# Attention in blocks of four tokens, with gated loads and three loads a pair on GpSimd, in a four-layer kernel

## The chip, the cores and the metric

The kernel runs on one core of a Trainium2 chip. The core has TensorE (PE: matrix products; PEld is its loading of stationary operands), VectorE (DVE), ScalarE (ACT), GpSimd (POOL) and SyncE (SP), each with an instruction queue of its own that runs in order, and 16 DMA engines that move data between HBM and the on-chip memory SBUF. Products land in PSUM, eight banks of 128 x 512 floats. The metric is device time in microseconds. All data is fp32.

## The reference

The input `x` is 64 sequences of 64 tokens with 256 features, 4,096 tokens in all. Four layers follow, each added to its input:

```python
# 0: two projections with weights scaled by the sequence's condition
down = relu(einsum('bsd,bdh->bsh', x, down_project * dg + db))
x = x + (einsum('bsh,bhd->bsd', down, up_project * ug + ub) + x)
# 1: a weight per sequence, of rank 30, made by a decoder
U = (mu @ W_dec + b_dec).reshape(B, 257, 30)
x = x + (x @ (U @ V)[:, :-1] + (U @ V)[:, -1:])
# 2: attention among the 16 heads of one token, q = k = v
kx = modulated_linear(x, ...).reshape(B, N, 16, 16)
A = softmax(einsum('bnhd,bnjd->bnhj', kx, kx) / 4)
x = x + modulated_linear(einsum('bnhj,bnjd->bnhd', A, kx).reshape(B, N, 256), ...)
# 3: norms with gathered gains, three state vectors, an MLP over six parts, a norm
x = x + mlp_ln(concat([w0*h, w1*t, w2*m, w3*n, w4*r, w5*s]), ...)
```

In layer 2 every token has its own 16 x 16 table of scores between its heads. So attention is 4,096 small products of 16 x 16 by 16 x 16, and the same number with the values.

## The kernel before

Layers 0, 1 and the keys of layer 2 go over chunks of 512 tokens (eight, `layers01`); attention and everything behind it go over pairs of 128 tokens, that is 256 (sixteen, called P; `attention` and `layers23`). Activations are kept with features in the partitions up to the keys (`xs`, `kT`).

**How attention is packed.** TensorE transposes the keys of a pair (`pt`, L721), ScalarE copies them twice into `kk` (L727 with feature ahead of head, L730 as they are), and SP writes both forms to HBM, `kd` (L736) and `vd` (L744). From there `fetch` brings them back in other arrangements:

- `kc` (L754) holds a row for each of 16 features and 8 groups of 32 tokens, 128 rows. ScalarE copies it into `kz`, where every token's 16 columns lie between zeros (L756).
- `kb` (L762, eight loads, one a group) is block-diagonal: the rows of group b are filled in block b only, and the other blocks stay zero. `vb` (L767, eight loads) is the same for the values.

A product of `kz`'s 32 columns for one g by `kb[:, :, g, :]`, 8 blocks of 16 columns, so takes eight tokens at once; two of them accumulate, since the 32 columns are a window that holds the tokens in one half (L789). This is `pS`: 32 products of 128 x 32 by 128 x 128 a pair, spread over the four 32-column groups of the array, four partitions' quarters of one PSUM bank. Of each product's output 16 rows count, and the accumulation fills both halves.

VectorE then takes the maximum over each row (L796) and subtracts it (L797), ScalarE takes the exponential (L798), VectorE sums (L799), inverts (L800), multiplies (L801) and transposes in 32 x 32 blocks into `at` (L803). `pv` is 32 products of `at`'s 32 columns by `vb[:, :, g, :]`, again 128 columns (L813), in two banks; ScalarE copies each into `av` (L818), and `av` goes to HBM (`ad`, 512 KB, L822) and comes back as `aT` with features in the partitions (L829). Rows that hold another token's product are left behind there. The tokens arrive in an order of their own, which `styleq` (L502) and the output's copy `ot` (L886) follow.

`kb` and `vb` are there once, `kz` twice. They lie in `kv`, which at the start holds layer 1's decoder (`W_dec`, six pieces); once the decoder is used up, GpSimd fills `kv` with zeros (L488, two halves).

**The norms.** `layers23` gathers rows of three tables with indirect loads on GpSimd (L856, six a pair) and loads `ei`, `tab` and `xr`, the parked residual, on SP (L861, L862, L871). Each of three norms a pair takes a power of -0.5 on GpSimd (L842), between a VectorE instruction (L841) and those that use it (L906, L920, L959).

**The start.** All weights are loaded once. SP issues nearly all of them in the order of their use, ScalarE the six pieces of the decoder. `pU` (L469, 60 products) makes the factor `U` from the decoder; VectorE adds the bias (L472).

**The order of instructions.** No engine chooses at run time. Every piece of work is a `step` with an engine, an estimated cost, what it reads and writes, and a rank; `Plan.order` plays the steps against a simple model of the engines and emits them in the order of their modelled starts. The rank is a base, by pair or chunk, plus a number for the step's stage (`LEAD`) and one by stage and pair (`SHIFT`). So a change of these two tables reorders every queue. A step whose buffer is still in use can't be placed earlier than the buffer's modelled release. On the chip, each instruction waits for what it needs, and all that stand behind it on its engine wait with it.

Of the kernel before, what the change touches and what calls it, by code (L numbers as in the profile page):

```python
# [19 lines left out]
CH = 512  # L20
# [41 lines left out]
class Plan:  # L62
# [6 lines left out]
    LEAD = {"down": 946.4, "fetch": 1090.6, "gather": 1168.5, "hidden": 1056.4, "keys": 938.1, "last": 1046.3,  # L69
            "load": 934.3, "load W1": 1568.6, "load W2": 1287.4, "load decoder": 1245.0, "load first": 604.2, "load ids": 902.1,  # L70
            "load keys": 911.3, "load states": 1260.1, "load up": 753.0, "mid": 546.9, "norm": 984.7, "out": 1165.7,
            "park": 927.1, "scores": 1120.2, "set W1": 1041.3, "set decoder": 215.9, "set down": 150.6, "set k": 952.6,
            "set o": 868.6, "set states": 1178.6, "turn": 1040.2, "up": 1091.5, "values": -313.8}


    SHIFT = {"down": (121.0, 0.0, -136.0, 0.0, 45.3, 0.0, 57.2, 0.0, 669.8, 0.0, 452.8, 0.0, 448.6, 0.0, 203.0, 0.0),
            "fetch": (-21.2, -95.4, 22.4, 39.5, 73.9, 129.8, -198.4, 143.2, 60.9, 236.7, -128.9, -10.1, -60.7, 22.7, -201.3, -74.5),
            "gather": (25.1, 20.6, -52.3, 44.9, 149.5, 295.4, 273.6, -73.2, 25.2, 4.2, 71.4, 347.0, 156.9, 181.1, 284.4, 233.7),
            "hidden": (-23.7, -102.8, 100.9, 97.4, -70.1, 56.9, 93.3, -244.5, -119.8, 73.4, -11.9, 193.5, 100.1, -16.4, -8.7, 2.5),
            "keys": (-138.5, 0.0, -157.5, 0.0, 320.2, 0.0, 194.1, 0.0, 169.5, 0.0, 259.2, 0.0, 207.7, 0.0, 209.6, 0.0),  # L80
            "last": (-49.6, -146.3, 100.1, 60.6, -162.7, -187.0, 32.8, 25.1, 68.0, -10.7, 96.6, -194.4, -61.8, 407.3, 397.6, 375.4),
            "load": (0.0, 0.0, 0.0, 0.0, 311.2, 0.0, 24.7, 0.0, -364.5, 0.0, 23.9, 0.0, 66.9, 0.0, 299.3, 0.0),
            "mid": (-25.3, 0.0, -351.6, 0.0, -179.2, 0.0, -1.1, 0.0, -6.1, 0.0, 131.7, 0.0, 213.3, 0.0, 249.5, 0.0),
            "norm": (-246.5, -272.7, -139.3, -283.8, -207.2, -15.7, -104.9, 40.1, -219.1, 16.5, -133.9, -101.4, -119.9, 129.5, 13.2, -265.9),
            "out": (75.9, 13.0, -112.7, -113.3, -174.2, 11.1, 82.9, 26.4, 125.1, -118.1, 220.2, -0.8, 136.4, 254.8, -8.3, 195.2),
            "park": (-302.5, 0.0, -53.5, 0.0, -775.7, 0.0, -547.9, 0.0, -550.1, 0.0, -359.8, 0.0, -152.5, 0.0, 238.3, 0.0),
            "scores": (-82.8, 70.4, 67.7, -137.7, -106.8, -38.2, 26.9, 83.3, 98.4, 82.9, 84.9, -0.6, 136.4, 144.2, 34.2, 171.0),
            "turn": (-82.0, 10.3, -20.8, -18.4, -23.5, -0.8, 77.8, 214.9, 84.7, 115.0, -41.3, 77.4, -122.1, 45.8, 69.3, 164.8),
            "up": (-344.7, 0.0, -102.1, 0.0, -238.6, 0.0, -224.7, 0.0, -115.4, 0.0, -84.9, 0.0, -54.9, 0.0, -53.0, 0.0),
            "values": (-74.2, 53.7, -70.1, -159.6, 81.8, 307.5, -59.3, -54.8, 80.6, -145.4, -166.2, -196.3, -101.8, -85.7, -218.8, 125.5)}  # L90
# [12 lines left out]
    @staticmethod  # L103
    def keys(things):
        out = []
        for t in things:
            if isinstance(t, tuple) and isinstance(t[0], Buf):
                out.append((t[0], t[1]))
            else:
                out.append((t, None))  # L110
        return out
# [142 lines left out]
def act(n):  # L254
    return 0.06 + n / 1220.0
# [3 lines left out]
def tile_kernel(ctx: ExitStack, tc: tile.TileContext, a: dict, out: bass.AP):  # L259
# [15 lines left out]
    BUFS = {"x": 3, "xr": 3, "pw": 2, "cg": 2, "mg": 2, "ei": 2, "oh": 2, "t4": 3, "kk": 2, "kc": 1, "act": 2, "E": 2,  # L275
            "aT": 2, "xt": 2, "ft": 2, "hs": 2, "y3": 2, "y1": 1, "mx": 2, "sm": 2, "tab": 2, "st": 2, "mv": 2, "rs": 2, "rsx": 2, "rsh": 2, "rsy": 2, "nmx": 2, "nmh": 2}
# [4 lines left out]
    def bank(name, tag="B"):  # L281
        return Buf(ps, tag, {"A": 2, "B": 3, "C": 2, "S": 1}[tag], [128, 512], name, turns=(tag == "A"))
# [35 lines left out]

    styleq = fixed("styleq", [128, 2, B // PB, 4, 2])
# [14 lines left out]
    kz = [fixed(f"kz{i}", [128, 32 * NG + 16]) for i in range(2)]  # L334

    kv = fixed("kv", [128, 2 * NG * 128])
    kb, vb = (kv[:, i * NG * 128 : (i + 1) * NG * 128].rearrange("p (b g j) -> p b g j", g=NG, b=8) for i in range(2))
    at_ = fixed("at", [128, 32 * NH + 16])


    def consts():
# [4 lines left out]
    step("POOL", 0.4, lambda: (nc.gpsimd.memset(neghalf, -0.5), nc.gpsimd.memset(V, 0.0), nc.gpsimd.memset(bigtab, 0.0),  # L346
                               nc.gpsimd.memset(at_[:, 32 * NH :], 0.0)),
         w=["neghalf", "V", "at0", "zeros"], rank=-107)
    step("POOL", 3.5, lambda: nc.gpsimd.memset(U, 0.0), w=["U"], rank=-108.5)
    for z in range(2):  # L350
        step("POOL", 1.0, lambda z=z: nc.gpsimd.memset(kz[z], 0.0), w=[f"kz{z}"], rank=-106)
# [5 lines left out]
    def load_x(c, rank):  # L357
        x = xs_[c] = sb("x", [128, 2, CH], f"x_{c}")
        step("SP", Plan.ISSUE, lambda: nc.sync.dma_start(x(), xTd[:, :, c * CH : (c + 1) * CH]),
             w=[(x, 0), (x, 1)], rank=rank, dma=4 * 128 * 2 * CH)  # L360
# [35 lines left out]
    load_x(1, -109.1)  # L396
# [3 lines left out]
    for i, (n, tag) in enumerate((("h", "ft"), ("t", "ft"), ("m", "fs"), ("n", "fh"), ("r", "aS"), ("s", "ot"))):  # L400
        W1r[n] = sb(tag, [128, 2, D], f"W1r_{n}")
    plan.stage = "load W1"
    for i, n in enumerate("htmnrs"):
        step("SP", Plan.ISSUE, lambda i=i, n=n: nc.sync.dma_start(W1r[n](), int_W1[i]), w=[W1r[n]], rank=-108.5 + 0.01 * i, dma=262144)
    plan.stage = "load states"
    load("cond64T", cond64T, a["cond64T"], -108.4)
    load("fsideT", fsideT, a["fsideT"], -108.4)
    rows_, w1_, w2_ = {}, {}, {}
    rowsd = a["rows"].rearrange("(m v) d -> m (v d)", m=3)
    for i, (m, kdim, t2, tr) in enumerate((("mem", C, "xt", "av"), ("noi", 64, "xt", "cg"), ("res", 32, "xh", "pw"))):  # L410
# [3 lines left out]
        step("SP", Plan.ISSUE, lambda m=m: nc.sync.dma_start(w1_[m](), a[f"{m}_W1"]), w=[w1_[m]], rank=-108.3, dma=1024 * kdim)  # L414
        step("SP", Plan.ISSUE, lambda m=m: nc.sync.dma_start(w2_[m](), a[f"{m}_W2"].rearrange("(k p) o -> p k o", p=128)),
             w=[w2_[m]], rank=-108.2, dma=262144)
        step("SP", Plan.ISSUE, lambda m=m, i=i: nc.sync.dma_start(rows_[m]()[0:B, 0 : 3 * D], rowsd[i].partition_broadcast(B)),
             w=[rows_[m]], rank=-108.1, dma=196608)
    betas = fixed("betas", [128, 3, 2, 8])
    load("betas", betas, a["betas"].rearrange("n (k p) e -> p n k e", p=128), -108.0)  # L420
    plan.stage = "load W2"
    load("W2", W2, a["int_W2"].rearrange("(k p) o -> p k o", p=128), -107.9)
    load("irow", irow, a["int_rows"].rearrange("n d -> (n d)").partition_broadcast(128), -107.8)
# [63 lines left out]
    for n, half in (("kb", 0), ("vb", 1)):  # L487
        step("POOL", 3.5, lambda half=half: nc.gpsimd.memset(kv[:, half * NG * 128 : (half + 1) * NG * 128], 0.0),  # L488
             w=[n] + [f"W_dec{i}" for i in range(NW)], rank=-104)


    for n in "ko":
# [8 lines left out]
        if n == "o":  # L501
            step("DVE", 1.0, lambda: [nc.vector.tensor_copy(  # L502
# [268 lines left out]
    def parts(n):  # L771
        return [f"{n}.{b}" for b in range(8)]
# [274 lines left out]
```

## Time and profile before

| | |
|---|---|
| median of nine runs | 489.71 us (480.35 to 496.4) |
| profiled execution | 484.41 us |
| its span, first to last instruction | 482.6 us |
| TensorE's granted clock, mean | 0.932 |
| packets moved by DMA | 192,668, 83.53 MB |
| DMA queue of SP (q1) | 51.6% of 16 engines' span |
| DMA queue of GpSimd (q0) | 15.9% |

The time of a run lies a little above the span. Lines of the profile name the source line, the engine and the operation, the tile written and those read. "Idle before" is the time for which the engine had nothing to do ahead of an instruction, with what ended it. SPq, ACTq and POOLq are the parts of those engines that issue DMAs; time there is issuing, not moving. A matrix product in fp32 appears as two records. The granted clock (PEclk) is a share of full speed.

### The profile page before, as it was taken

How to read it: one execution, taken by the hardware profiler on the slowest of the kernel's cores; microseconds unless marked ns; L12 is line 12 of the kernel's file. 1: busy time of each engine (PE TensorE's matmuls, PEld its weight loads, DVE VectorE, ACT ScalarE, POOL GpSimd, SP SyncE). 2: the span in 40 equal slices, each digit the busy share in tenths (PEclk: the TensorE clock that was granted, in tenths of full speed). 3: DMA queues.
4: the chain of work that ended last, by engine and by line, in shares of the span. 5: the costliest groups of instructions: out<-in, count | busy, mean ns of one | idle time of the engine just before them, and what ended most of it. 6: DMA issues, size and time to landing. Idle time of an engine off the chain costs nothing.

```text
span 482.6 us, 11060 instructions
## 1 busy us (share of the span) xinstructions
PE 417.3 (86%) x4026; PEld 317.2 (66%) x4026; DVE 309.4 (64%) x668; ACT 296.9 (62%) x875; POOL 154.7 (32%) x164
## 2 busy tenths in 40 slices
PE   4989949967889899989989989998899968999890
PEld 2876624654666677678757667777667757888770
DVE  0568894560865576597758756858774863876642
ACT  1303916519648964889179737994598855776530
POOL 5552030000155133044613540335132723355110
PEclk9957977978799999999999999999899997999996
DMA  8998578467596789659866897588767867765000
GB/s 278 299 235 271 118 132 225 124 98 166 87 185 202 238 164 214 155 149 228 199 191 122 227 199 184 147 228 148 152 197 232 159 152 196 190 207 157 23 22 22
DMA packets 192668, 83.53 MB, mean 173 GB/s; under 512 B 159819, under 2 KB 174119, under 8 KB 192615
## 3 DMA queue, kind: packets, MB, share of 16 engines
q1 hardware_dynamic: 184679, 57.81, 51.6%
q0 software_dynamic: 6656, 20.98, 15.9%
q10 hardware_dynamic: 1280, 4.05, 2.3%
q8 instruction: 32, 0.52, 0.5%
q14 instruction: 21, 0.17, 0.1%
HBM read 56.91 MB, written 25.89 MB: 172 GB/s over the span
## 4 chain that ended last, share of the span: by engine, by line
PE 51%; ACT 14%; DMA 9%; DVE 9%; SPq 9%; issue 5%; POOL 1%; POOLq 0%; another core or an unknown queue 0%; ACTq 0%; DVEq 0%
PE ph L943 16%; PE pv L813 5%; PE pS L789 4%; ACT kT L710 4%; PE po L883 4%; PE pk L707 4%; SPq L762 3%; PE pq L951 3%; PE pU L469 3%; DMA kc<-kd 3%; ACT junk L834 2%; PE pz L688 2%; SPq L744 2%; ACT ot L886 2%; SPq L767 1%
## 5 line engine op out<-in xcount | busy, mean ns | idle before, releaser
L842 POOL TENSOR_TENSOR rs_x<-rs_x,neghalf 128x2 f32<-128x2 f32 x16 | 13.0, 811 | 111.4 <-DVE rs_x L841 110.3
L886 ACT ACTIVATE ot<-po,cols,demod_o 128x64 f32<-128x64 f32 x128 | 41.0, 429 | 10.6 <-PE po L883 10.6
L856 POOL DMA_INDIRECT mg<-in_ms_tab,ids x32 | 33.4, 1044 | 34.4 <-PE pfs L928 20.1
L710 ACT ACTIVATE kT<-pk,cols,demod_k 128x64 f32<-128x64 f32 x128 | 39.6, 442 | 7.8 <-PE pk L707 7.8
L856 POOL DMA_INDIRECT pw<-in_pw_tab,ids x32 | 34.9, 1090 | 17.8 <-PE pfh L928 10.5
L789 PE MATMUL pS<-kv,kz 128*32 128x128 f32 x1024 | 34.6, 288 | 4.2 <-DMA kv<-vd 3.5
L856 POOL DMA_INDIRECT cg<-in_cg_tab,ids x32 | 32.7, 1021 | 16.4 <-issue 7.5
L813 PE MATMUL pv<-kv,at 128*32 128x128 f32 x1024 | 34.8, 283 | 3.6 <-DVE at L803 2.4
L883 PE MATMUL po<-aS,w_o 128*128 128x256 f32 x128 | 32.6, 400 | 5.4 <-DVE aS L877 5.4
L943 PE MATMUL ph<-ft,W_t 128*128 128x256 f32 x128 | 34.6, 394 | 2.5 <-ACT ft L931 2.5
L707 PE MATMUL pk<-xs,w_k 128*128 128x512 f32 x64 | 33.8, 671 | 3.3 <-issue 2.3
L789 PEld LDWEIGHTS pS<-kv,kz 128*32 128x32 f32 x1024 | 29.5, 116 | 9.8 <-issue 8.6
L813 PEld LDWEIGHTS pv<-kv,at 128*32 128x32 f32 x1024 | 28.3, 113 | 11.0 <-issue 4.0
L943 PE MATMUL ph<-fh,W_h 128*128 128x256 f32 x128 | 33.5, 385 | 1.9 <-ACT fh L931 1.7
L951 PE MATMUL pq<-W,hs 128*128 128x256 f32 x128 | 32.2, 390 | 2.8 <-ACT hs L946 2.5
L943 PE MATMUL ph<-fs,W_s 128*128 128x256 f32 x128 | 33.1, 381 | 1.1 <-ACT fs L931 1.1
L842 POOL TENSOR_TENSOR rs_h<-rs_h,neghalf 128x2 f32<-128x2 f32 x16 | 13.1, 819 | 65.3 <-DVE rs_h L841 65.1
L943 PE MATMUL ph<-xr,W_x 128*128 128x256 f32 x128 | 33.1, 381 | 0.0
L656 ACT ACTIVATE t<-pu,ugT 128x64 f32<-128x64 f32 x128 | 27.5, 378 | 7.8 <-PE pu L651 4.0
L883 PEld LDWEIGHTS po<-aS,w_o 128*128 128x128 f32 x128 | 24.7, 199 | 10.7 <-issue 7.5
L756 ACT COPY kz<-kc 128x512 f32<-128x512 f32 x16 | 10.0, 627 | 33.6 <-DMA kc<-kd 33.5
L943 PEld LDWEIGHTS ph<-ft,W_t 128*128 128x128 f32 x128 | 22.7, 189 | 10.6 <-ACT ft L931 3.6
(228 smaller groups left out, 953.2 us busy)
## 6 DMA issues: line engine op xcount, KB each, us to landing
ad<-av SPq DMA_DIRECT2D x16, 512.0 KB
x<-in_xT SPq DMA_DIRECT2D x8, 512.0 KB
xd<-x SPq DMA_DIRECT2D x8, 512.0 KB
xr<-xd SPq DMA_DIRECT2D x16, 256.0 KB
kd<-kk SPq DMA_DIRECT2D x32, 128.0 KB
vd<-kk SPq DMA_DIRECT2D x64, 64.0 KB
kc<-kd SPq DMA_DIRECT2D x16, 256.0 KB
kv<-kd SPq DMA_DIRECT2D x128, 32.0 KB
```

What stands on the lines that cost most here:

```text
L469: mm(pU()[:, k * B : (k + 1) * B], Wd[:, c, k0 + k, :], condT, start=True, stop=True)
L656: nc.scalar.activation(t1()[:, d, h * 256 + b * S : h * 256 + (b + 1) * S], pu[h]()[:, d * 256 + b * S : d * 256 + (b + 1) * S], AF.Copy, ...
L707: step("PE", 1.82, lambda o=o: [mm(pk[o](), wT["k"][:, k, o * 128 : (o + 1) * 128], xs()[:, k, :], start=(k == 0), stop=(k == 1)) for k in ...
L710: nc.scalar.activation(kT()[:, o, b * S : (b + 1) * S], pk[o]()[:, b * S : (b + 1) * S], AF.Identity, scale=demod["k"][:, o, b0 + b : b0 + ...
L789: mm(pS()[32 * cc : 32 * cc + 32, r * 128 : (r + 1) * 128], kzt[:, g * 32 + 16 : g * 32 + 48] if h == 0 else kzt[:, g * 32 : g * 32 + 32], ...
L813: mm(pv[h]()[32 * q : 32 * q + 32, r * 128 : (r + 1) * 128], at_[:, c0 : c0 + 32], vb[:, :, q * 8 + h * 4 + r, :], start=True, stop=True)
L842: step("POOL", 1.25, lambda: nc.gpsimd.tensor_tensor(rs(), rs(), neghalf[:, 0:2], ALU.pow), r=["neghalf"], w=[rs], rank=rank)
L856: step("POOL", 1.35, lambda dst=dst, tab=tab, i=i, t=t: nc.gpsimd.indirect_dma_start(out=dst()[:, t, :], out_offset=None, in_=a[tab], in_o ...
L883: step("PE", 1.74, lambda: [mm(po()[:, o * PT : (o + 1) * PT], wT["o"][:, k, o * 128 : (o + 1) * 128], aS()[:, k, :], start=(k == 0), stop ...
L886: step("ACT", 1.16, lambda o=o: [nc.scalar.activation(ot()[:, o, b * S : (b + 1) * S].rearrange("p (z s) -> p z s", z=2), po()[:, o * PT : ...
L943: mm(dst(), W1[n][:, k, o * 128 : (o + 1) * 128], rhs()[:, k, :], start=False, stop=(n == "h" and k == 1))
L951: step("PE", 0.90, lambda t=t: [mm(pq()[:, t * D : (t + 1) * D], hs()[:, k, t * 128 : (t + 1) * 128], W2[:, k, :], start=(k == 0), stop=(k ...
```

## The change

**Attention.** A product still takes eight tokens, now as four blocks by two parities: the 32 stationary columns are the 16 heads of a token of each parity side by side (`kz[g]`), and the rows of `kd` are ordered feature, parity, group, so that a key row belongs to one parity. The same `kc` row set is copied twice into `kz`, each time scaled by a mask (`tmask`, a new small input) that is one for rows of that parity and zero for the other. `kb` has four blocks of 16 columns, so a product has 64 moving columns, and none accumulates. The values carry a seventeenth column of ones (`vk`, written once at the start), so that `pv`'s seventeenth column is the sum of the exponentials: 68 moving columns a product. The exponential is taken after the transpose, in two halves of 64 partitions, straight into `at`, whose other places stay zero from the start. The sum, its inverse and the product on VectorE go; instead VectorE inverts column 17 of `pv` and multiplies while it moves `pv` into `av`, which ScalarE did. `av` and `ad` halve (256 KB). `kb`, `vb` are there twice, by the parity of the pair. Keys are fetched by four loads of 32 rows instead of eight of 16. ScalarE writes `kT` in the order of tokens that the blocks want, so `styleq` and the reordering in `ot` go.

**The gate.** A one-element copy on GpSimd reads the fifth piece of `W_dec`; the loads of `x_1`, W1, the states, W2 and the rows of the last norm, and later chunks of `x`, wait for it.

**GpSimd's loads.** `ei`, `tab` and `xr` are issued by GpSimd instead of SP.

**The planner.** All numbers of `LEAD` and `SHIFT` are new, PSUM bank S now takes its tiles in turn as bank A does, and the kv memset is in four parts.

```diff
-    kz = [fixed(f"kz{i}", [128, 32 * NG + 16]) for i in range(2)]
-    kv = fixed("kv", [128, 2 * NG * 128])
-    kb, vb = (kv[:, i * NG * 128 : (i + 1) * NG * 128].rearrange("p (b g j) -> p b g j", g=NG, b=8) for i in range(2))
-    at_ = fixed("at", [128, 32 * NH + 16])
+    kz = [fixed(f"kz{i}", [128, NG, 2, NH]) for i in range(2)]
+    WK, WV = 4 * NG * HD, 4 * NG * (HD + 1)
+    kv = fixed("kv", [128, 2 * WK + 2 * WV])
...
+    vk = [fixed(f"vk{i}", [128, 2, NH, HD + 1]) for i in range(2)]
+    tmask = fixed("tmask", [128, 2])
+    at_ = fixed("at", [128, NG, 2, NH])
...
+    GATE = 4
+    step("POOL", 0.2, lambda: nc.gpsimd.tensor_copy(W1r["h"]()[:, 0, 0:1], W_dec[:, GATE * 1280 : GATE * 1280 + 1]),
+         r=[f"W_dec{GATE}"], w=[W1r["h"], "gate"], rank=-109)
...
+    load_x(1, -109.1, ["gate"])
...
-    for n, half in (("kb", 0), ("vb", 1)):
-        step("POOL", 3.5, lambda half=half: nc.gpsimd.memset(kv[:, half * NG * 128 : (half + 1) * NG * 128], 0.0),
+    for n, lo, w in (("kb0", 0, WK), ("vb0", 2 * WK, WV), ("kb1", WK, WK), ("vb1", 2 * WK + WV, WV)):
+        hi = lo + w
+        step("POOL", 1.8, lambda lo=lo, hi=hi: nc.gpsimd.memset(kv[:, lo:hi], 0.0),
...
-        step("ACT", act(512), lambda: nc.scalar.copy(view(kz[z], [[32, NG], [1, NH]], 16), kc().rearrange("p (g h) -> p g h", h=NH)),
-             r=[kc], w=[f"kz{z}"], rank=rank)
-        for b in range(8):
...
+        for t in range(2):
+            step("ACT", act(512), lambda t=t: nc.scalar.activation(kz[z][:, :, t, :], kc(), AF.Copy, scale=tmask[:, t : t + 1]), r=[kc, "tmask"],
+                 w=[f"kz{z}.{t}"], rank=rank)
+        for b in range(4):
...
-            for r in range(4):
-                for h in range(2):
-                    for cc in range(4):
-                        g = h * 16 + r * 4 + cc
-                        mm(pS()[32 * cc : 32 * cc + 32, r * 128 : (r + 1) * 128],
-                           kzt[:, g * 32 + 16 : g * 32 + 48] if h == 0 else kzt[:, g * 32 : g * 32 + 32],
-                           kb[:, :, g, :], start=(h == 0), stop=(h == 1))
+            for g8 in range(8):
+                for cc in range(4):
+                    g = g8 * 4 + cc % 2 * 2 + cc // 2
+                    mm(pS()[32 * cc : 32 * cc + 32, g8 * 64 : (g8 + 1) * 64], kz[z][:, g].rearrange("p a h -> p (a h)"), kb[z][:, :, g, :],
+                       start=True, stop=True)
...
-        step("ACT", act(512), lambda: nc.scalar.activation(E(), E(), AF.Exp, scale=1.0 / 4.0), w=[E], rank=rank, table="exp")
-        step("DVE", vec(512), lambda: nc.vector.tensor_reduce(sm(), E(), AX.X, ALU.add), r=[E], w=[sm], rank=rank)
-        step("DVE", 0.39, lambda: nc.vector.reciprocal(sm(), sm()), w=[sm], rank=rank)
-        step("DVE", vec(512), lambda: nc.vector.tensor_tensor(E(), E(), rep(sm(), NH), ALU.mult), r=[sm], w=[E], rank=rank)
-        step("DVE", vec(512), lambda: nc.vector.transpose(at_[:, 0 : 32 * NH], E().rearrange("p g j -> p (g j)")), r=[E], w=["at"], rank=rank)
+        Et = sb("E", [128, NG, NH], f"Et_{P}")
+        step("DVE", vec(512), lambda: nc.vector.transpose(Et().rearrange("p g i -> p (g i)"), E().rearrange("p g j -> p (g j)")), r=[E], w=[Et], rank=rank)
+        for h in range(2):
+            step("ACT", act(512), lambda h=h: nc.scalar.activation(
+                at_[64 * h : 64 * h + 64, :, h, :], Et()[64 * h : 64 * h + 64], AF.Exp, scale=1.0 / 4.0), r=[Et, "at"], w=[f"at.{h}"], rank=rank, table="exp")
...
-        for z in range(2):
-            step("ACT", act(512), lambda z=z: nc.scalar.copy(
-                av()[:, :, :, z],
-                pv[z]().rearrange("p (r c l d) -> p d l r c", r=4, c=4, d=HD)), r=[pv[z]], w=[(av, z)], rank=rank)
+            step("DVE", 0.25, lambda h=h, pvv=pvv: nc.vector.reciprocal(sm()[:, h * 16 : (h + 1) * 16], pvv()[:, :, HD]), r=[pv[h]], w=[(sm, h)], rank=rank)
+            step("DVE", vec1(256), lambda h=h, pvv=pvv: nc.vector.tensor_tensor(
+                view(av(), [[1, 8], [16, 2], [32, HD]], h * 8), pvv()[:, :, 0:HD].rearrange("p (s y) d -> p s y d", y=2),
+                rep(sm()[:, h * 16 : (h + 1) * 16].rearrange("p (s y) -> p s y", y=2), HD), ALU.mult), r=[pv[h], (sm, h)], w=[(av, h)], rank=rank)
...
-        step("SP", Plan.ISSUE, lambda: nc.sync.dma_start(ei(), a["ei"][:, P * PT : (P + 1) * PT]), w=[ei], rank=rank, dma=45056)
-        step("SP", Plan.ISSUE, lambda: nc.sync.dma_start(tb(), tabd()[P]), r=[tabd], w=[tb], rank=rank, dma=45056)
+        step("POOL", 1.1, lambda: nc.gpsimd.dma_start(ei(), a["ei"][:, P * PT : (P + 1) * PT]), w=[ei], rank=rank, dma=45056)
+        step("POOL", 1.1, lambda: nc.gpsimd.dma_start(tb(), tabd()[P]), r=[tabd], w=[tb], rank=rank, dma=45056)
...
-        step("SP", Plan.ISSUE, lambda: nc.sync.dma_start(x(), xd().rearrange("(k p) t -> p k t", p=128)[:, :, half * PT : (half + 1) * PT]),
+        step("POOL", 1.2, lambda: nc.gpsimd.dma_start(x(), xd().rearrange("(k p) t -> p k t", p=128)[:, :, half * PT : (half + 1) * PT]),
```

## The prediction

> **What bounds the kernel now.** I read the page's busy times first, then its chain of waits by engine and line.
>
> ```profile
> PE 417.3 (86%) x4026; PEld 317.2 (66%) x4026; DVE 309.4 (64%) x668; ACT 296.9 (62%) x875; POOL 154.7 (32%) x164
> ...
> PE 51%; ACT 14%; DMA 9%; DVE 9%; SPq 9%; issue 5%; POOL 1%; POOLq 0%; another core or an unknown queue 0%; ACTq 0%; DVEq 0%
> PE ph L943 16%; PE pv L813 5%; PE pS L789 4%; ACT kT L710 4%; PE po L883 4%; PE pk L707 4%; SPq L762 3%; PE pq L951 3%; PE pU L469 3%; DMA kc<-kd 3%; ACT junk L834 2%; PE pz L688 2%; SPq L744 2%; ACT ot L886 2%; SPq L767 1%
> ```
>
> TensorE is busy 86% of 482.6 us, but only half of the chain that ended last is TensorE; the rest changes from engine to engine and to SP's queue (SPq). So I split the span into stages.
>
> ```profile
> core 0: us, PE busy (x) PEld busy (x) DVE busy (x) ACT busy (x) POOL busy (x), PEclk, DMA share, GB/s
> 0.00:34.00 34.00, 24.03 (x164) 21.30 (x164) 13.75 (x26) 5.29 (x19) 17.75 (x23) 0.86 0.94 276
> 34.00:100.00 66.00, 54.96 (x513) 34.52 (x513) 48.26 (x104) 32.75 (x98) 10.13 (x9) 0.84 0.68 171
> 100.00:440.00 340.00, 309.02 (x3213) 238.10 (x3210) 227.57 (x490) 243.13 (x709) 119.97 (x123) 0.96 0.76 180
> 440.00:482.60 42.60, 29.29 (x145) 23.28 (x143) 19.78 (x51) 15.78 (x51) 6.83 (x9) 0.92 0.13 40
> ```
>
> The first stage is loads (DMA 94% busy). From 100 to 440 us TensorE is 91% busy, ScalarE 72%, VectorE 67%, DMA 76%: TensorE bounds this stage, with 31 us of idle time. The tail has no attention in it. Third view, the chain in order of time (start, length, what):
>
> ```profile
> 25.24 4.06 DVE aw L532
> 29.38 4.53 PE pU L469 x20
> ...
> 134.44 1.02 PE py L678 x32
> ...
> 143.55 1.88 PE pv L813 x64
> ...
> 194.15 1.89 PE pS L789 x64
> ```
>
> A product here makes two records, so pS is 32 products of 128 columns in four column groups, and py 16 products of 64 columns in two.
>
> **TensorE's part.** pS: 64 records in four groups are 16 rounds, 1.89/16 = 0.118 us a round of 128 columns. py: 32 records in two groups are 16 rounds, 1.02/16 = 0.064 us a round of 64 columns. The changed scores have the same 32 products and weight loads, at 64 columns, none accumulating: 16 x 0.064 = 1.02 us, 0.87 saved. The values go from 128 to 68 columns: 16 x 0.064 x 68/64 = 1.09 us, 0.79 saved. Together 1.66 us a pair, 26.6 us over 16 pairs. That is TensorE's time, not the path's: on the chain pv and pS hold 5.2% and 4.0%, 44.4 of their 69.4 us. The same cut (46% of pS's 19.3, 42% of pv's 25.1) leaves 19.5 us on the path. No row has four groups at 64 columns; the bounds are 0.064 and 0.118 us a round, a saving of 26.6 or 0. I take the first, since py has the same columns. What decides is whether TensorE can be fed so fast: the 64 weight loads and 64 products of a pS come 128 in 1.89 us now, 14.8 ns each, and would have to come in 1.02, 8 ns each:
>
> ```profile
> 416.35 0.16 PEld L789 LDWEIGHTS pS<-kv,kz 128*32 128x32 f32 x8 [0.17 <-issue]
> 416.35 0.32 PE L789 MATMUL pS<-kv,kz 128*32 128x128 f32 x4
> ```
>
> This timeline was cut at 416.405: eight weight loads and four products began in 0.055 us, 4.6 ns each. A burst is fast enough; that a long run is, no row shows.
>
> The Trainium skill has a rule against this step: "TensorE: Matmul & The Clock Gate", section "Wait — 56ns, not 53.3ns?", says that starts of matmuls never come closer than about 25 ns, however few the columns. The burst above shows closer starts across column groups, but the averages, 1.89/64 = 29.5 ns in pS and 1.02/32 = 31.9 ns in py, stay above that floor. By it (an estimate) 64 records take 1.6 us, 15% less, and the chain would lose 6.7 us instead of 19.5.
>
> **VectorE and ScalarE.** Per pair, VectorE loses the sum (0.684), the 128x32 reciprocal (0.350) and the product with it (0.690), and gains two 128x16 reciprocals from PSUM (between 0.17 for 128x1, L536, and 0.35 for 128x32; take 0.25) and two products of 256 elements (0.42 by L683; at most 0.69 by L801): -1.72 + 1.34 = -0.4 us, 6 us in all. ScalarE loses two copies of pv (0.606 each) and gains a second exponential (0.632; each covers 64 partitions with as many elements) and a second masked key copy (0.627): +0.05 us a pair. Both hide in idle time. The four copies of styleq (0.5 us) go, and the early memsets cover 2,112 columns instead of 2,096: nothing. In the changed order ScalarE's table loads go from 26 to 33:
>
> ```profile
> L798 ACT ACT_TABLE_LOAD x11 | 14.1, 1283 | 0.2
> ...
> L818 ACT COPY av<-pv 128x512 f32<-128x512 f32 x32 | 18.8, 606 | 17.5 <-PE pv L813 17.2
> ```
>
> Seven times 1.283 is 9 us on ScalarE; at its 14% of the chain +1.5 us, all 9 if ScalarE becomes the bound (it would be near 253 of some 313 us, 81%).
>
> **SP's and GpSimd's queues.** Between 114.3 and 118.9 us the chain runs through SP alone, one key load after another at 0.59 us. Keys now come in four loads instead of eight, and three loads a pair (0.37, 0.41 and 0.39 us: L861, L862, L871) leave SP: 2.4 + 1.2 = 3.5 us a pair. If a load of twice the rows takes twice the issue, the 2.4 is gone; but kc, 128 rows, is issued in 0.43 us, so I keep 0.59. L762 holds 3.5% of the chain, 17 us; half of it is 8.5, and I count half of that, -4, as the next thing late there is the transfer itself. Key and value buffers twice over also let loads begin before the last pair's products are done; TensorE waits for these loads 3.7 us in all now, so I count nothing, and keep -6 for the range.
>
> GpSimd gains 48 issues. Bounds: SP's 0.39 us and 1.60 us, the longest indirect load; take 1.04, an indirect load's mean. That is 50 us on an engine 32% busy. Its queue is in order, and a load there waits for its buffer: xr for TensorE's last read, ei for oh, tab for ph. Behind it stand the 48 powers of the norms (L842), for which VectorE waits, then ScalarE and TensorE. Today they stand behind a load 29 times in 48, in the new order 37 times. GpSimd sat idle 111, 65 and 42 us ahead of the three powers, waiting for VectorE, and this idle time hides the issues; I count the eight more, a quarter of 1.04 us each, +2 us, and up to 50 if the cover goes.
>
> The skill's "DMA: Bandwidth & Descriptors", section "Issuing engine by pattern", gives plain loads to SP; its first-byte times (1 us against 0.6) would make 48 x 0.4 = 19 us, an estimate, if all of it were exposed. The rows agree in direction, and no GpSimd plain load is in this trace.
>
> Transfers: ad halves (4.2 MB less; at q1's 57.81 MB for 51.6% of the span, 18 us of all engines), aT has twice the pieces (16,384 more; at q1's mean, 249 x 16 / 184,679 = 21.6 ns, +22 us). These cancel; DMA is 76% busy in the main stage.
>
> **The start.** The gate on GpSimd (L407 of the changed code) waits for the fifth piece of the decoder; behind it stand the memsets of kv and the gathers, and SP holds x_1, aw, the states, W1 and W2 behind it: 4.35 MB. Some 5.9 MB go ahead of it; at 276 GB/s that is 21 us, and the rest lands by 37. First uses now are 36.3 (x_1), 43.0 (states), 47.9 us (W1): covered by little more than 5 us. The gain: pU ran 50 records in 5.85 us, so its 120 need 14.0; from 11.5 with 2.1 us of other products between, they could end at 27.6 and ended at 33.9. VectorE's scaling of aw took 4.06 us there beside GpSimd's 3.5 us memset of kv. In the new order it stands three groups of pU later, and the memsets are halves. Between 0 and 6.3, I take -4.
>
> **Sum:** -19.5 - 4 - 4 + 1.5 + 2 = -24, a span of 458.6 us. The profiled execution took 484.41 us, 1.8 around its span, so 460.4; the median of nine runs, 489.71, is 1.0109 times it: **465 us**.
>
> **Rivals.**
> (a) TensorE gains nothing: it takes records at 29 to 32 ns whatever the columns; both averages speak for it, the burst against it. Then -4.5: a span of 478.1, a run of 479.9, a median of 485 (482 to 488).
> (b) More comes: all 26.6 us, 6.3 at the start, 8.5 at SP, 6 from the second buffers less 3.5: -44, 445. Against it: half of the chain is not TensorE, and its clock (0.96, and 0.84 between 34 and 100) may fall with more gaps.
> (c) **Slower:** GpSimd's queue. Loads wait at its head for buffers, and the powers behind them come late. 48 issues at 1.04 us; the gains without it are 26 us, so it decides from 26/48 = 0.54 us exposed for each; at 1.04, +24: 506.6, 508.4, 514. For it: the 36 us that GpSimd's gathers now wait for TensorE and VectorE (mg 20.1, pw 10.5, cg 5.5). Against: the idle time above.
> (d) The work is done faster and the path moves to ScalarE and the transfers: half the gain: 470.6, 472.4, 478.
>
> **How the numbers follow.** My forecast (456 to 474) 0.52, (d) 0.15, (b) 0.10, (a) 0.12, (c) 0.11. One per cent, 4.9 us, is about what a measurement can tell from no change: bounds 484.8 and 494.6. (a) falls half on each side of the lower. Faster 0.83, same 0.06, slower 0.11. The range leaves out (c), the lower half of (b) and the upper quarter of (a), 0.19: 449 to 486.
>
> **What would show it.** pS near 1.02 us for 64 records and TensorE busy near 391 us: right; pS still at 1.6 or more: (a). DVE waiting for rs from POOL over 20 us (now 4.9 for rs_x): (c). pub ending near 30 us: the start. ScalarE over 85% busy between 100 us and the tail: (d). The prediction fails if TensorE's idle time grows by what its work shrinks.

## The result and the profile after

The changed kernel takes 540.21 us (median of 20 runs, 534.77 to 555.4) where the kernel before takes 488.07 (62 runs): 1.112 times as long, interval 1.109 to 1.115. Some executions of most kernels here take 1.5% or more longer than its fastest; ratios here and below compare the others alone, while a time in us is the median of all. The prediction was 465, faster. The profiled execution took 548.69 us, 8 over its median; nothing below rests on that difference.

The page's busy times and DMA queues of the changed kernel (queues: packets, megabytes, share of 16 engines):

```profile
PE 427.5 (78%) x4026; PEld 321.1 (59%) x4026; DVE 305.6 (56%) x680; ACT 312.1 (57%) x882; POOL 188.5 (34%) x215
...
DMA packets 206412, 79.86 MB, mean 146 GB/s; under 512 B 175515, under 2 KB 188407, under 8 KB 206359
...
q1 hardware_dynamic: 196119, 48.50, 59.6%
q0 software_dynamic: 8960, 26.62, 20.3%
...
PE 6%; DVE 1%; ACT 1%; issue 0%; POOLq 0%; ACTq 0%; DVEq 0%
```

No compute engine is above 78%, and fewer bytes than before move more slowly. The last line is the chain; it breaks off 48 us before the end and says nothing of the main stage. So the stages have to tell, in windows of the changed kernel:

```profile
core 0: us, PE busy (x) PEld busy (x) DVE busy (x) ACT busy (x) POOL busy (x), PEclk, DMA share, GB/s
0.00:34.00 34.00, 27.04 (x128) 24.20 (x128) 9.73 (x17) 5.08 (x18) 13.78 (x22) 1.00 0.85 252
34.00:100.00 66.00, 56.13 (x418) 36.33 (x419) 44.28 (x96) 27.20 (x75) 20.39 (x20) 0.88 0.72 151
100.00:500.00 400.00, 307.32 (x3309) 231.20 (x3307) 227.33 (x507) 260.85 (x732) 141.57 (x158) 0.87 0.92 147
500.00:546.90 46.90, 37.05 (x176) 29.36 (x175) 24.28 (x60) 18.96 (x60) 12.79 (x16) 0.91 0.18 52
```

The main stage, as cut here, ends 60 us later. TensorE is idle 93 us of it (31 before), the DMA engines are 92% busy instead of 76% and move 147 GB/s instead of 180: they work longer for less. TensorE's granted clock in the stage was 0.87 (0.96 before; 0.95 in rows64 below). Who waits for the transfers in the changed kernel, directly or behind the copy `kz`, by waits (total us, times, longest):

```profile
ACT kz L768 <- DMA kc<-kd: 73.6, 12, 16.5
...
PEld pS L800 <- ACT kz L768: 14.7, 3, 7.1
...
PE pS L800 <- DMA kv<-kd: 11.2, 3, 4.3
```

The first of these lines in the kernel before:

```profile
ACT kz L756 <- DMA kc<-kd: 33.5, 8, 10.0
```

The products on TensorE did become shorter. Groups of the kernel before (busy us, mean ns of one, idle before):

```profile
L813 PE MATMUL pv<-kv,at 128*32 128x128 f32 x1024 | 34.8, 283 | 3.6 <-DVE at L803 2.4 <-issue 0.7 <-ACT hs L946 0.2
...
L789 PE MATMUL pS<-kv,kz 128*32 128x128 f32 x1024 | 34.6, 288 | 4.2 <-DMA kv<-vd 3.5 <-issue 0.5 <-DMA kv<-kd 0.2
```

Groups of the changed kernel, and one pS on its timeline, near the forecast 1.02 us (six of the sixteen took 1.10, seven 1.9 or more):

```profile
L800 PE MATMUL pS<-kv,kz 128*32 128x64 f32 x1024 | 23.8, 255 | 23.9 <-DMA kv<-kd 11.2 <-ACT kz L768 9.9 <-DVE E L807 1.8
...
L823 PE MATMUL pv<-kv,at 128*32 128x68 f32 x1024 | 22.4, 241 | 7.7 <-ACT at L812 5.1 <-ACT hs L954 1.6 <-DVE nm_x L856 0.5
...
L828 DVE TENSOR_TENSOR av<-pv,sm 128x256 f32<-128x256 f32 x32 | 18.9, 600 | 1.0
...
L812 ACT ACT_TABLE_LOAD x14 | 18.0, 1283 | 0.2
```

```profile
205.56 1.10 PE L800 MATMUL pS<-kv,kz 128*32 128x64 f32 x64
```

The DMA packets of the trace, sorted by size (the sum over 16 engines is the time they occupy all of them), name the suspect. In the changed kernel a store of `vd` moves rows of 16 values and a one: 68 bytes, at a pitch of 68 (a row begins 68 bytes after the one before it).

```
kernel   bytes  packets  mean ns  99th ns  sum/16 us
before      64  131,200     10.2              83.4   (half of it kd, half vd)
after       64   65,664     13.2       98     54.3   (kd)
after       68   65,536     25.8      376    105.6   (vd)
```

All packets together, without the loading of instructions, took 336 us of the 16 engines before and 448 after. A mean hides how this time is spread: half of the 68-byte pieces took 12 ns or less, little more than the 11 of the pieces before, but 6.7% took over 50 ns, 208 on average, and these hold 57 of the 106 us (before: 0.02%). It is a small share of long stalls, not a price that every piece pays.

### The profile page after: what moved, and what is told of

Same layout as the page of the kernel before. It is cut to its first block, busy times and chain, and to the rows that moved or that the text cites. A ratio compares the mean times of both kernels' runs of the same rounds, so it can differ in the third digit from the quotient of the medians.

```text
span 546.9 us, 11027 instructions
## 1 busy us (share of the span) xinstructions
PE 427.5 (78%) x4026; PEld 321.1 (59%) x4026; DVE 305.6 (56%) x680; ACT 312.1 (57%) x882; POOL 188.5 (34%) x215
## 5 line engine op out<-in xcount | busy, mean ns | idle before, releaser
L768 ACT ACTIVATE kz<-kc,tmask 128x512 f32<-128x512 f32 x32 | 21.9, 716 | 73.6 <-DMA kc<-kd 73.6
L951 PE MATMUL ph<-fh,W_h 128*128 128x256 f32 x128 | 36.0, 411 | 16.6 <-ACT fh L939 16.6
L865 POOL DMA_INDIRECT mg<-in_ms_tab,ids x32 | 36.9, 1154 | 25.8 <-PE pfs L936 19.3
L800 PE MATMUL pS<-kv,kz 128*32 128x64 f32 x1024 | 23.8, 255 | 23.9 <-DMA kv<-kd 11.2
L865 POOL DMA_INDIRECT pw<-in_pw_tab,ids x32 | 33.6, 1049 | 22.6 <-PE pfh L936 10.2
L951 PEld LDWEIGHTS ph<-fh,W_h 128*128 128x128 f32 x128 | 24.8, 203 | 22.6 <-ACT fh L939 19.0
L800 PEld LDWEIGHTS pS<-kv,kz 128*32 128x32 f32 x1024 | 20.3, 133 | 29.8 <-issue 15.1
L959 PEld LDWEIGHTS pq<-W,hs 128*128 128x128 f32 x128 | 24.6, 201 | 22.1 <-ACT hs L954 15.9
L951 PE MATMUL ph<-fs,W_s 128*128 128x256 f32 x128 | 36.6, 412 | 0.2 <-ACT fs L939 0.2
L714 PE MATMUL pk<-xs,w_k 128*128 128x512 f32 x64 | 30.0, 604 | 2.4 <-DVE xs L708 2.4
L880 POOL DMA_DIRECT2D xr<-xd x16 | 12.5, 781 | 51.4 <-PE ph L951 27.0
```

What stands on the lines that cost most here:

```text
L714: step("PE", 1.82, lambda o=o: [mm(pk[o](), wT["k"][:, k, o * 128 : (o + 1) * 128], xs()[:, k, :], start=(k == 0), stop=(k == 1)) for k in ...
L768: step("ACT", act(512), lambda t=t: nc.scalar.activation(kz[z][:, :, t, :], kc(), AF.Copy, scale=tmask[:, t : t + 1]), r=[kc, "tmask"], w= ...
L800: mm(pS()[32 * cc : 32 * cc + 32, g8 * 64 : (g8 + 1) * 64], kz[z][:, g].rearrange("p a h -> p (a h)"), kb[z][:, :, g, :], start=True, stop ...
L865: step("POOL", 1.35, lambda dst=dst, tab=tab, i=i, t=t: nc.gpsimd.indirect_dma_start(out=dst()[:, t, :], out_offset=None, in_=a[tab], in_o ...
L880: step("POOL", 1.2, lambda: nc.gpsimd.dma_start(x(), xd().rearrange("(k p) t -> p k t", p=128)[:, :, half * PT : (half + 1) * PT]), r=[xd] ...
L951: mm(dst(), W1[n][:, k, o * 128 : (o + 1) * 128], rhs()[:, k, :], start=False, stop=(n == "h" and k == 1))
```

## The experiments

Theories: **R**, the 68-byte rows clog the DMA engines; **O**, the new order of the steps costs; **G**, GpSimd's loads block its queue (rival c of the prediction). Times beside one another are of the same chip; ratios are to the kernel before, whose medians lay between 484 and 494 us. Where a ratio has no interval, it rests on one or two runs of the variant.

### Are the rows of 68 bytes the cause?

**rows64** takes the ones out of `vd`; the ones are left out of the computation with them.

```diff
-vd = Buf(dram, "vd", 2 * NC, [2, 2, 2 * NH, 32, HD + 1], ...)
+vd = Buf(dram, "vd", 2 * NC, [2, 2, 2 * NH, 32, HD], ...)
...
-src = bass.AP(src.tensor, src.offset, [[4 * src.ap[0][0], 32], [HD + 1, 2 * NH], [1, HD + 1]])
+src = bass.AP(src.tensor, src.offset, [[4 * src.ap[0][0], 32], [HD + 1, 2 * NH], [1, HD]])
```

> The changed kernel with only 16 values in each row of vd: pieces of 64 bytes at a pitch of 64, as before the change, and the value loads bring 1,024 bytes instead of 1,088. The order and every instruction on the engines stay; the products still take 17 columns, the 17th being a value of the next block, so the ones are left out and the quotient is not the softmax's. Theory R (the rows of 68 bytes): 65,536 pieces took 25.8 ns each, 105.6 us of all 16 DMA engines; at the 13.2 ns that a piece of 64 bytes takes in the same run they take 54, so 52 us of DMA time go, the DMA share between 100 and 500 us falls from about 0.93 to about 0.80, ScalarE's wait for kc falls from 73.6 us towards 33, and the time falls from 540 to between 460 and 490. Theory O (the new order of the steps) and theory G (GpSimd's three loads): the order is the same, the time stays within 10 us of 540.

Measured: **465.78 us** where the kernel before took 484.20; ratio 0.967 (0.959 to 0.975). With every engine's instructions and their order unchanged, the ratio falls from 1.112 to 0.967, some 71 us, and TensorE is busy 395.2 us instead of 427.5. The main stage of rows64 in its window, and its wait for `kc`:

```profile
100.00:400.00 300.00, 266.89 (x2981) 200.75 (x2979) 204.27 (x460) 237.29 (x668) 134.34 (x146) 0.95 0.79 179
```

```profile
ACT kz L768 <- DMA kc<-kd: 18.9, 6, 7.6
```

131,200 pieces of 64 bytes took 10.1 ns again, and all packets together 332 us. Of the 116 us between this and the changed kernel's 448, the pieces of `vd` are 105.6 - 41.6 = 64; the other 52 are packets of other transfers that took longer beside them (64 bytes 10.1 to 13.2 ns, 2,048 bytes 100.9 to 119.8, 4,096 bytes 224 to 266; the value loads, 1,024 to 1,088 bytes, 54 to 73). R holds; O cannot be a large part, since the order is the same and the kernel is now faster than before.

**before68** puts the suspect into the kernel before: 16 values and a neighbour's element, which no product reads (so the two halves of `kk` change places, and the value loads grow from 2,048 to 2,176 bytes).

```diff
-vd = Buf(dram, "vd", 2 * NC, [8, NH, NG, HD], ...)
+vd = Buf(dram, "vd", 2 * NC, [8, NH, NG, HD + 1], ...)
...
-[[4 * k.ap[0][0], 32], [HD, 2 * NH], [1, HD]]
+[[4 * k.ap[0][0], 32], [HD, 2 * NH], [1, HD + 1]]
...
-vb[:, :, q * 8 + h * 4 + r, :]
+vb[:, :, q * 8 + h * 4 + r, 0:HD]
```

> The kernel before with rows of 68 bytes in vd (16 values and one element of the neighbour, which no product reads), value loads of 2,176 bytes instead of 2,048, and nothing else changed: the suspected cost alone, without the new order and without GpSimd's loads. Theory R: the same 65,536 pieces go from about 10 to about 26 ns, 64 us more of all DMA engines, on a kernel whose DMA engines are 76% busy: the time rises from 488 to between 515 and 560. Theories O and G: it stays within 5 us of 488.

Measured: **569.21 us**, ratio 1.167 (1.154 to 1.180). Four bytes a row cost some 81 us, without anything else of the change, and the median lies a little above the 515 to 560 us expected; the pieces took 22.6 ns (99th percentile 331). ScalarE's wait for `kc` in this kernel:

```profile
ACT kz L756 <- DMA kc<-kd: 111.0, 13, 18.8
```

**sploads** lets SP issue the three loads again, at their place in the order.

```diff
-nc.gpsimd.dma_start(ei(), ...)   # and tb(), x()
+nc.sync.dma_start(ei(), ...)
```

> The changed kernel with the three loads a pair (ei, tab, xr) issued by SP again, at the same place in the order; the rows stay at 68 bytes. Theory R: GpSimd's queue is not the cause; within 10 us of 540. Theory G (loads block the queue in which the powers of the norms stand): GpSimd was 29 us in issues and DVE waited 13.4 us for its powers, 8.1 before; the time falls by 15 to 50 us, to between 490 and 525. Theory O: within 10 us of 540.

Measured: **555.12 us**, ratio 1.139 where the changed kernel has 1.112, some 13 us more; R allowed 10. G falls: GpSimd's loads do not slow the kernel, they help it.

### Length or place?

Three kernels hold the ones in `vb` from the start and load 64-byte pieces into every 17 floats; they differ in the layout of `vd`: in its stores, and in where the loads of `vb` read.

```diff
 # preset:    rows at a pitch of 64 bytes, 64 written
 # preset128: rows at a pitch of 128 bytes, 68 written
 # preset_u:  rows at a pitch of 68 bytes, 64 written
-vb[z][b * 16 : (b + 1) * 16, b % 4].rearrange("p (t g) d -> p t (g d)", t=2)
+vb[z][b * 16 : (b + 1) * 16, b % 4, t * 16 : (t + 1) * 16, 0:HD]     # for t in range(2)
+nc.gpsimd.tensor_copy(vb[z][:, :, :, HD], rep(vmask, NG))             # once
```

> Complete attention with rows of 64 bytes: vd holds 16 values a row at a pitch of 64, the ones stand in vb from the start (set once on GpSimd from a mask) and the value loads, 16 a pair instead of 8, bring pieces of 64 bytes into every 17 floats of vb, so that the products of 68 columns stay as they are. Against rows64: 65,536 reads of 64 bytes at some 10 ns for 4,096 of 1,024 bytes at 54 ns, 41 - 14 = 27 us more of all 16 DMA engines, and 128 more issues on SP at 0.42 us, 54 us of its queue. If the writes of 68 bytes alone were the trouble, 470 to 490; if 64-byte pieces as such are slow wherever a line is not moved as a whole on both sides, above 500.

> As preset, but the rows of vd stand at a pitch of 128 bytes, and 68 bytes of each are written (the 17th float is not read again). Every piece begins on a multiple of 64 bytes and no two share a line of 64. Theory L (a write that covers part of a line is slow, whoever else writes there): the 68-byte pieces take 20 ns or more on average, as in the changed kernel, and the time is 40 us or more above preset. Theory S (slow only where two rows share a line of 64 bytes and are written by different engines): the pieces take 11 to 14 ns and the time is within 15 us of preset.

> As preset, but the rows of vd stand at a pitch of 68 bytes, and 64 bytes of each are written and read. The length is that of preset, only the place is not: nearly every piece lies across two lines of 64 bytes, and neighbouring rows share them. Theories L and S both: the writes are slow, 20 ns or more on average, and the time is 40 us or more above preset. If it is the length of 68 alone (a piece of 64 and a rest of 4), the time stays within 15 us of preset.

Measured: **544.63, 589.49 and 633.76 us** (486.52 before); ratios 1.122, 1.216 and 1.306.

```
kernel     bytes  pitch  packets  mean ns  99th ns
preset        64     64  196,736     10.3       15   (stores of kd and vd, loads of vb)
preset128     64         131,200     11.5       33   (kd, loads)
preset128     68    128   65,536     14.3       89   (vd)
preset_u      64         196,736     16.1      194   (all; for vd an estimate of about 25, if the rest took 11.5)
```

The length alone is not it: 64 bytes at a pitch of 68 are the worst. The place alone is not all: 68 bytes that begin on a multiple of 64 and share no 64 bytes with another row still cost 45 us over preset, though each takes only 14.3 ns; packets of 4,096 bytes went from 242 to 291 ns beside them. So neither S (slow only where rows share 64 bytes) nor L (slow wherever 64 bytes are written in part) held as put: pieces of 64 bytes on multiples of 64 are cheap, 68 bytes cost more and slow others, and rows that share 64 bytes cost most. Three things stay open. No run stores 64 bytes at a pitch of 128, so the pitch may have a part in the 45 us. In preset_u the loads of `vb` lie at a pitch of 68 too, and the estimate puts nothing down to them. And the runs do not tell units of 64 bytes from units of 32. Issue to landing of the transfers, preset128 and then preset_u (last number, median us):

```profile
vd<-vk SPq DMA_DIRECT2D x64, 68.0 KB, 6.3
...
kc<-kd SPq DMA_DIRECT2D x16, 256.0 KB, 5.6
```

```profile
vd<-vk SPq DMA_DIRECT2D x64, 64.0 KB, 9.4
...
kc<-kd SPq DMA_DIRECT2D x16, 256.0 KB, 10.4
```

In rows64 the same two take 5.2 and 4.1 us. The loads of `kc`, which the scores wait for, are hit by stores of another buffer.

The Trainium skill, "DMA: Bandwidth & Descriptors", section "Specifications", puts the line at 512 bytes, below which a transfer is read, modified and written. All these pieces lie below it, so it does not tell them apart; the runs do: 64 bytes on multiples of 64 took 10 ns, 68 bytes at a pitch of 68 took 25.8.

preset itself came out 55 us above the top of its range, with fast pieces and its DMA engines 69 to 78% busy between 100 and 500 us. Its 256 value loads hold SP 131 us (75 in rows64), and SP waited 30.6 us for earlier loads to land before it could issue these; that this is the cause was not tried by itself. Its time is in the range above 500 us that was expected for slow pieces, and its pieces were not slow: the time of the pieces alone does not give the time of a kernel.

### Does the harm go through SP's queue?

Theory **Q** says so: SP was 363 us in its issues in the changed kernel and 308 in rows64, with the same 428 issues. **after_vdact** and **sums_vdact** move the stores of `vd` to ScalarE; **sums** is rows64 made complete by products against a mask of ones.

```diff
 # sums: for each block of four products of 64 columns
+mm(pv[h]()[32 * q : 32 * q + 32, 256 + s4 * 4 : 260 + s4 * 4], at_[:, g8 * 4 + q]..., vmask, start=True, stop=True)
 # the two _vdact kernels
-nc.sync.dma_start(vd()[cc, e]..., src)
+nc.scalar.dma_start(vd()[cc, e]..., src)
```

> Rows of 64 bytes as in rows64, and the sums complete: each value product of 64 columns is followed by one of 4 columns, with the same weights, against a fixed mask of ones. This adds 64 TensorE records of 4 columns a pair; at 0.01 to 0.03 us each, 0.6 to 2 us a pair, of which half is on the path: 5 to 16 us over rows64. Theory R: 465 to 505. Theories O and G: 540 to 560.

> The changed kernel, rows of 68 bytes and all, with the four stores of vd a pair issued by ScalarE instead of SP; the order is the same. SP was 363 us in its issues in the changed kernel and 308 in rows64, with the same 428 issues: the slow writes hold up the queue behind them. Theory Q (the harm goes through SP's queue: stores wait in it until the engines take them, and the key loads behind them come late): the 74.5 us of the stores and some 40 us of other lengthened issues leave SP, and the time falls from 540 to between 480 and 515. Theory E (the DMA engines themselves are the bound, whoever issues): 530 to 560, and ScalarE, held at its issues, may make it worse.

> sums (64-byte rows, complete) with the four stores of vd a pair issued by ScalarE: 66 us leave SP, which stands at 302 us in all and is 65 to 92% busy with issues between 100 and 400 us; ScalarE takes some 0.7 us for each, 45 us on an engine 66% busy. If SP's queue holds sums back, 465 to 478 instead of 482; if TensorE (86% busy) does, within 4 us of 482; if ScalarE's queue becomes the bound, above 488.

Measured: sums **481.94 us** (484.20 before), after_vdact **572.58** and sums_vdact **502.39** (494.38 before); ratios 0.986, 1.147 and 1.016, from two runs, one and two. In after_vdact SP is only 53 to 66% busy with issues in each 100 us between 200 and 500 us (70 to 80% in the changed kernel) and ScalarE's wait for `kc` falls to 32.4 us, yet nothing is won; the 68-byte pieces still take 21.9 ns, and the DMA engines stay as busy, as its window shows:

```profile
200.00:300.00 100.00, 86.88 (x932) 64.26 (x928) 63.25 (x135) 68.53 (x182) 39.13 (x45) 0.91 0.91 167
```

Theory Q falls as the whole cause: with the pressure off SP's queue, the harm remains. That it is then the DMA engines that bound the kernel is argued from their 91%, not shown; preset was as slow as the changed kernel with 72 to 73% in each 100 us. The test is not clean either, since the move does harm of its own: sums_vdact is 1.6% over the kernel before, sums 1.4% under. sums also prices TensorE: its 1,024 more records raise TensorE's busy time from 395.2 to 408.0 us, and the ratio from 0.967 to 0.986, some 9 us. Most of what is added to TensorE shows.

### Where the gain comes from once the rows are mended

**rows64_nogate** frees the gate, **rows64_sp** gives SP the loads, **rows64_sp_nogate** does both and so leaves the blocks of four and the new order; **before_pool** moves the loads alone, in the kernel before. The three rows64 kernels leave the ones out.

```diff
-nc.gpsimd.tensor_copy(W1r["h"]()[:, 0, 0:1], W_dec[:, GATE * 1280 : GATE * 1280 + 1])
+nc.gpsimd.tensor_copy(free, ones[:, 0:1])                       # nogate
...
-nc.gpsimd.dma_start(ei(), ...)   # and tb(), x()
+nc.sync.dma_start(ei(), ...)                                    # sp; the reverse in before_pool
```

> rows64 without the gate: the copy on GpSimd writes a float of its own and waits for nothing, so SP's early loads begin when their turn comes; the order is the same. As in rows64 the ones are left out. The prediction gave the gate 4 us (0 to 6.3): by it 470 (466 to 472), and pub ends later than in rows64. If the gate gave nothing, within 2 us of 466; if it holds the early loads back, below 464.

> rows64 (the ones left out) with ei, tab and xr issued by SP again, at their place in the order: 48 issues at some 0.45 us, 22 us on SP. The prediction's terms for this move were -4 (SP) and +2 (GpSimd): by them 468. If SP's queue is a bound beside TensorE, most of the 22 us show: 476 to 490.

> rows64 with the loads on SP and without the gate: what is left of the change is the attention in blocks of four alone (with 64-byte rows and without the ones) and the order. Taken singly, the gate was worth 5 to 8 us and the loads on GpSimd 9 to 17. If the shorter products give the 19.5 us of the prediction on the path: 468 to 474 where the kernel before is at 488 to 490. If they give nothing because SP's queue is the bound beside TensorE: 482 to 492.

> The kernel before with its three loads a pair (ei, tab, xr) issued by GpSimd, at their place in the order, and nothing else changed: 21 us of issues leave SP, whose issues take 347 us in all and which is 83 to 93% busy with them between 100 and 400 us. By the prediction's terms 484 to 486 instead of 488; if SP's queue bounds this kernel beside TensorE, 470 to 480; if the loads block GpSimd's queue (rival c), above 490.

Measured, as ratios to the kernel before:

```
rows64            0.967 (0.959 to 0.975)   465.78 us
rows64_nogate     0.977 (0.971 to 0.983)   473.92
rows64_sp         0.986 (0.966 to 1.005)   482.76
rows64_sp_nogate  0.982 (0.975 to 0.989)   481.78
before_pool       0.981 (0.963 to 0.998)   483.95
```

Blocks of four, with the new order, give 1.8%, 9 us (5 to 12). The loads on GpSimd give 1.9%, 9 us, in the kernel before and in rows64, and 0.5% without the gate. Taking the gate away costs 1.0%, 5 us, where GpSimd has the loads, and nothing that can be seen where SP has them. The parts don't add up, and but for the blocks of four the intervals are about as wide as the parts: of the loads, 1.9% is plus or minus 1.8 in the kernel before and 2.1 in rows64; of the gate, 1.0% is plus or minus 1.0.

### A version that beats both

**dmajor** writes the values from `kT`, where features are in the partitions and a feature's tokens lie side by side.

```diff
-vd = Buf(dram, "vd", 2 * NC, [2, 2, 2 * NH, 32, HD + 1], ...)
+vd = Buf(dram, "vd", 2 * NC, [8, NH, HD, 2 * 16], ...)
...
-nc.scalar.copy(vk[p][:, :, :, 0:HD]..., pt()...)
+[nc.scalar.copy(vk[p][:, o].rearrange("p y e t g -> p y t g e"), kT()[:, o, ...]...) for o in range(2)]
...
-nc.sync.dma_start(vd()[cc, e].rearrange("h g d -> g h d"), src)                  # four a pair
+nc.sync.dma_start(vd()[:, cc * 8 : cc * 8 + 8].rearrange("b h d g -> (h d) b g"), # two a pair
+                  vk[p][:, cc].rearrange("p y e t g -> p (y e) (t g)"))
...
-vb[z][:, :, q % 2 * 16 + q // 2 * 8 + g8, :]
+vb[z][:, :, :, q % 2 * 16 + q // 2 * 8 + g8]
+nc.gpsimd.tensor_copy(vb[z][:, :, HD, :], rep(vmask, NG))                        # once
```

> A complete version without the rows of 68 bytes and without products for the sums: the values go to vd from kT, where a partition holds one feature and its tokens lie along it, so that a piece is 32 tokens of one feature, 128 bytes on a multiple of 128 (32,768 pieces instead of 65,536); vb holds the tokens of a feature side by side, the ones are a 17th row of it, set once, and the value loads bring 2,048 bytes a piece. Stores of vd go from four a pair to two. The order on TensorE, VectorE and GpSimd is that of the changed kernel. If the place and length of the pieces is the whole harm: at 13.1 ns a piece (the 128-byte reads of aT in rows64) the stores take 27 us of all engines instead of 41 in rows64, SP loses 32 issues, and the time is rows64's 466 or up to 8 us less, 458 to 468. If the products suffer from columns 128 bytes apart in vb, 470 to 490, with pv's records longer than 0.22 us. If something else of the change costs besides the rows, above 490.

Measured: **462.33 us**, ratio 0.942 (0.936 to 0.948) to the kernel before, with the sums in it. The order of TensorE, VectorE and GpSimd, the blocks, the gate and GpSimd's loads are those of the changed kernel, so together with rows64 and before68 nothing but the rows is left to blame for the slowdown. 65,536 packets of 128 bytes (`vd` and `aT`) took 13.5 ns. Its main stage, in a window, and its value products, a group (the profiled execution took 12 us more than the median):

```profile
100.00:420.00 320.00, 295.29 (x3268) 224.25 (x3264) 223.81 (x496) 257.30 (x716) 141.92 (x155) 0.97 0.74 176
```

```profile
L826 PE MATMUL pv<-kv,at 128*32 128x68 f32 x1024 | 34.4, 294 | 4.7 <-ACT at L815 3.1
```

TensorE is 92% busy in the stage again, although `pv` got no cheaper than it was with 128 columns (34.8 us).

## Why the prediction was wrong, step by step

**Transfers, "these cancel": the step that failed.** It counted `ad` and `aT` and left out `vd`. What it counted did cancel: `ad` went from 21.6 to 15.3 us of all engines, `aT` from about 18.5 to 27.4. The 65,536 pieces that grew from 64 to 68 bytes were never priced; against rows64 they took 64 us more themselves, other packets took 52 more beside them, and they pushed the DMA engines from 76 to 92% of the main stage. The prediction gave no bound to an operation of which the trace before shows no row, so no rival held this either: its slower rival was (c). Its own last sign came true: TensorE's idle time in the main stage grew, by 62 us.

**TensorE.** The size was right: 64 records of a pS in 1.10 us (1.02 forecast, 1.89 before) in eleven of rows64's sixteen, TensorE busy 395.2 us in rows64 (391 forecast, 417.3 before). Rival (a) falls, and so does the floor of about 25 ns between starts that the Trainium skill states ("TensorE: Matmul & The Clock Gate", section "Wait — 56ns, not 53.3ns?"): 1.10/64 is 17 ns a record across four column groups. The part on the path was mis-sized: 9 us (5 to 12) with the blocks of four and the new order, where the forecast read 19.5 off the chain's shares.

**SP and GpSimd.** The -4 stood for the key loads and the three other loads together. The move of the three loads alone gave about -9 us with its cost on GpSimd (before_pool; -1 to -18), and exposed blocking on GpSimd did not come: VectorE's waits for the three powers were 13.4 us in all, and sploads was slower. SP's issues fill 83 to 93% of each 50 us of the kernel before between 100 and 400 us, by the sum of its issues. The 2.4 + 1.2 us a pair were about right (the key loads' issues fell from 78.7 to 41.3 us in rows64, 2.3 a pair; before_pool took 1.0 a pair off SP); the prediction then took a quarter of the 17 us that the chain gave to them.

**The start.** 5 us for the gate (0 to 10), where 4 was forecast, but not by the way described: pub began at 27.2 us in rows64 and at 27.7 without the gate (33.8 before). In the profile of the changed kernel, which has the order of rows64, it began at 41.2, before the first store of `vd` was issued at 69.1; so neither the order nor the rows set this time, and what does stays open. With the gate TensorE worked 53.4 us between 34 and 100 us, without it 47.6.

**ScalarE and VectorE.** 28 table loads ahead of the exponentials and `hs` took 36 us of ScalarE; whether all of it was hidden no run tells. ScalarE was 79% busy between 100 and 400 us in rows64, under the 85% that would have shown (d). The product with the reciprocals took 0.600 us, not 0.42: 5.8 us on VectorE, for which no compute engine waited (SP waited 9.3 us for `av` in rows64).

**The sum.** 465 against 489.71 was a ratio of 0.950; the change without its rows of 68 bytes stands at 0.967. The rest of the forecast was thus 8 us too hopeful, and its one missing term some 71 (1.112 less 0.967).

## What to carry to other kernels

A scatter's pieces, by these runs, belong on multiples of 64 bytes in length and place: check length and pitch of every short store that a change touches, and price it as a new operation even when only 4 bytes are added. Where a sentinel or a column of ones is wanted, set it once in SBUF, and look for a layout in which the long run is what is stored. A queue that is 85% busy with issues may be a second bound beside the busiest engine: taking three loads a pair off it gave about 9 us, but moving the stores of `vd` to ScalarE cost more than it freed, so try the move before counting on it.

## What the runs showed of the hardware

- Stores took 10 ns each on average at 64 bytes on a pitch of 64, 14.3 at 68 on 128, an estimated 25 at 64 on 68 and 25.8 at 68 on 68. In the last half took 12 ns or less and one in a hundred over 376, and packets of 2,048 and 4,096 bytes took 19% longer beside them than in rows64. Why, no run shows.
- Products whose moving columns lie 128 bytes apart took 294 ns a record on average in dmajor, against 241 with columns side by side in the changed kernel (230 in rows64), and `pv` 34.4 us instead of 22.4. The Trainium skill, "SBUF — State Buffer", section "Door 1: The DMA port swizzle (why `[64,N]` ≈ `[32,N]`)", says that each access crossing to a new line of 16 bytes pays a penalty; the direction agrees.
- The same stores issued by ScalarE instead of SP cost 3% (sums_vdact against sums, two runs each), although SP had been the fuller queue.
